# A four-layer gated cross-attention kernel: layer 1's table order turned ahead of the last shared products, and layer 1's last additions moved at the seam to layer 2

## The chip, the cores and the metric

The program runs on one core of a Trainium2 chip. A core has a matrix engine (TensorE, in the profile PE for the products and PEld for the loads of their weights), a vector engine (VectorE, DVE), a scalar engine (ScalarE, ACT), a general engine (GpSimd, POOL) and an engine that only issues transfers here (SyncE, SP). Each takes its instructions in order from its own queue; semaphores order the engines among each other. Transfers (DMA) are started by SP, and the indirect ones, whose addresses come from a table, by POOL. The metric is the device time of one execution in microseconds (us); of three runs the median counts.

## What is computed

Tokens `x` (8 sequences of 256, each token 512 numbers, f32) go through four layers. Each has a cross-attention to `ctx` and a feed-forward part, each behind a layer norm and scaled by the tanh of a gate:

```
x = x + tanh(g_xattn[l]) * xattn_l(layernorm(x), ctx)
x = x + tanh(g_ffn[l])   * ffn_l(layernorm(x))          # l = 0, 1, 2, 3
```

The change lies in layer 1's feed-forward part and at its border with layer 2's attention. These are, cut to what matters:

```
# layer 1, feed-forward: 64 experts, 8 of them for each token, one shared expert for all
def _route(x):                      # scores, the best 4 of 8 groups, the best 8 of their experts
    ...
    return topk_idx, topk_w * 2.5
oh  = one_hot(topk_idx.reshape(-1), 64)
pos = cumsum(oh, 0) - oh            # the place of each choice in its expert's list
buf[e, pos] += x[row]               # tokens gathered by expert
y   = einsum(silu(buf @ w_gate) * (buf @ w_up), w_down)
out = scatter_add(y * weight) + (silu(x @ sh_gate) * (x @ sh_up)) @ sh_down

# layer 2, attention, by sequence of 256 tokens; q = layernorm(x), k = v = ctx
scaled = einsum('bsd,bse->bde', q, k) / sqrt(512)
out    = einsum('bde,bse->bsd', softmax(scaled, axis=1), v)
```

## The kernel before

The 2048 tokens stay on the chip the whole time, as 16 tiles `xt[0..15]` of 128 tokens; four tiles are a block (four blocks, two sequences each). The program is written in the order of the computation, engine by engine; a scheduler lays out each engine's queue from that order, priorities, and explicit edges. `behind(one, other, reason)` is such an edge: `one` is put behind `other`.

*Ahead of the experts (middle, from L646).* For each block of layer 1 the attention runs in two batches (`attend1`, L833); it calls `step(n)` at many places, which moves the routing of earlier token pairs on and issues up to `n` table writes. A "pair" `q` is two tiles; there are eight (0 to 7). `route1(q)` (L969) computes scores, ranks and a payload `pay` (token number and weight) for each of two tiles and eight choices: the payload's weights come from sixteen `hit` products (L1064) on VectorE, and then sixteen `table` writes are pending (L1078). `write(n)` (L945) issues pending writes, each one an indirect DMA on POOL (L950) behind a given matrix product. The table holds, by expert and place, token and weight. The last pair, 7, also computes the order in which the experts come (`ranked`, `ordered`), in which the weights of the experts (`w`, 960 KB for a pair of experts, and `wd`) are then loaded by SP.

The norm of a block (`stats_of` L151, `normed` L169) takes VectorE's statistics, then `rstd` on POOL (L166), then `xn` on VectorE (L174); TensorE turns `xn` over (`tr_f`, L188).

The shared expert (`shared1`, L1087) of a block is 8 products each for gate (`shg`), up (`shu`) and remainder (`shr`), whose products on VectorE give `shT` (L1104; the remainder's two halves L1110), and then 16 products `shd` (L1121) whose results VectorE adds to `x` (`add_scaled`, L221). Blocks 0 to 2 are done here, with pair 7's routing and the pending writes between their steps: three writes at each step (loop at L1162). When all writes are out, POOL waits until they have landed and reads the table in the experts' order (`rows`, L1177); TensorE turns the rows (`who_ps`, L1193, put behind the last shared product), VectorE makes token numbers of them (`who`, L1197, put behind the last shared addition), and POOL gathers the first tokens by them (`xg`, L1213). The expert's first products, `gu`, need the gathered and turned tokens (`tr_xg` on TensorE L188, `eb` on VectorE L102). The experts follow, 112 tiles of gathered tokens, some 500 us. Their results are scattered by token into two buffers.

*Behind the experts.* Block 3's shared expert runs at the end (`end`, L1336). `combine` (L1344) loads the two experts' sums of each tile (`more`, 256 KB, SP) and adds them to `x` on VectorE (L1352): 32 additions. The `more` tiles lie in a ring of eight buffers, so a load waits until an earlier addition has released its buffer. Then layer 2 (`back`, L1552): for sequence `b` the load `kxvs` of 512 KB (L1363), `ctxTc` (1 MB, L91) for a block, the norm of the tokens (`a2`), products `s` of the scores, softmax, products `o`, and additions to `x`. SP issues its loads in order; `behind(... "not before it in the queue")` puts `kxvs` and `ctxTc` behind loads of `more`, and the loads `p` (weights of layer 2's feed-forward part, 512 KB) come after.

Of the kernel before, what the change touches and what calls it, by code (L numbers as in the profile page):

```python
# [11 lines left out]
F32 = mybir.dt.float32  # L12
# [3 lines left out]
ALU = mybir.AluOpType  # L16
# [4 lines left out]
P = 128  # L21
# [5 lines left out]
BLK = 512  # L27
NB = NT // BLK
TB = BLK // P
# [17 lines left out]
def flamingo_kernel(ctx: ExitStack, tc: tile.TileContext, a):  # L47
    nc = tc.nc
# [102 lines left out]
    def stats_of(ts_, name, after=()):  # L151
# [14 lines left out]
        nc.gpsimd.tensor_tensor(out=rstd[:, :n], in0=ve[:, :n], in1=mhalf[:, :n], op=ALU.pow)  # L166
        yield ts_, mv, rstd

    def normed(stats, name, after=()):  # L169
        ts_, mv, rstd = stats  # L170
        out = []
        for i, t in enumerate(ts_):
            xn = xnp.tile([P, C], F32, tag="xn", name=f"xn_{name}_{i}")
            one = nc.vector.tensor_scalar(xn, xt[t], mv[:, i, 0:1], rstd[:, i : i + 1], ALU.subtract, ALU.mult)  # L174
            for other in after:
                behind(one, other, "the scores first")
            out.append(xn)
        return out

    def norm(blk, name):  # L180
# [35 lines left out]
    def mmtile(name):  # L216
        return mm.tile([P, BLK], F32, tag="mm", name=name)

    def add_scaled(i, ps, scale):

        return nc.vector.scalar_tensor_tensor(xt[i], ps, scale, xt[i], ALU.mult, ALU.add)  # L221
# [424 lines left out]
    def middle():  # L646
        with ExitStack() as st:
# [185 lines left out]
            def attend1(blk, one_step):  # L833
# [24 lines left out]
                for bb in range(BLK // S):  # L858
                    nm = f"{blk}_{bb}"
                    kf, V = context1(blk, bb, K, step) if bb else first  # L860
                    if blk == NB - 1 and bb:
                        step = lambda n: one_step(n, True)
                    qf = b8.tile([P, NH // 2, S], F32, tag="b8", name=f"qf_{nm}")
                    for cc in range(2):
# [63 lines left out]
                    for nt in range(2):  # L928
                        aoT = t2.tile([P, KC, P], F32, tag="t2", name=f"aoT_{nm}_{nt}")
                        aoTs.append(aoT)  # L930
                        transpose4(aoT, aos[nt].rearrange("p h d -> p (h d)"), f"ao_{nm}_{nt}")
                        step(1)
                    for nt in range(2):
                        ps = mmtile(f"wo1_{nm}_{nt}")
                        matmul_k(ps, [aoTs[nt][:, k, :] for k in range(KC)], [wo[:, k, :] for k in range(KC)])
                        i = blk * TB + bb * 2 + nt
                        add_scaled(i, ps, tg[:, 1:2])
                        step(2 if nt == 0 else 0)
                    done.append(blk * (BLK // S) + bb)

            tokens, done, counted = {}, [], []
# [27 lines left out]
            def route1(q):  # L969
# [91 lines left out]
                hit = sm.tile([P, E1], F32, tag="hit", name=f"hit{q}", bufs=2)  # L1061
                for i in range(2):
                    for j in range(K1):
                        nc.vector.scalar_tensor_tensor(  # L1064
                            hit, key[:, i, :], key8[:, i, j : j + 1], w[:, i, :], ALU.is_equal, ALU.mult,
                            accum_out=pay[:, i, j, 1:2],
                        )
                    nc.vector.tensor_scalar(
                        pay[:, i, :, 1], pay[:, i, :, 1], den[:, i : i + 1], None, ALU.mult
                    )  # L1070

                    for j in range(K1):
                        pending.append((row_i[:, i, j : j + 1], pay[:, i, j, :]))
                    if q == 2 * NB - 1:
                        write(len(pending))
                    if i == 0 and q == 2 * NB - 1:
                        expert = ranked(run[:, 1, :], sel[:, 1, :])
                    yield  # L1078
                if q == 2 * NB - 1:
                    ordered(expert)  # L1080
                    yield

            I1R = I1 - P
            rows_of = (slice(0, I1R), slice(FD, FD + I1R))
            rest1 = rows_of[1]

            def shared1(blk, shgu):  # L1087


                xnT = [tokens[blk][:, k, :] for k in range(KC)]  # L1090
                hT = [t2.tile([P, BLK], F32, tag="t2", name=f"shT{blk}_{h}") for h in range(2)]
                act = [t2.tile([P, BLK], F32, tag="t2", name=f"sha{blk}_{h}") for h in range(2)]

                def products(name, cols):
                    ps = mmtile(f"{name}{blk}")
                    n = cols.stop - cols.start
                    matmul_k(ps[:n, :], [shgu[:, k, cols] for k in range(KC)], xnT)
                    return ps

                pg = products("shg", slice(0, P))  # L1100
                nc.scalar.activation(act[0], pg, AF.Silu)
                yield
                pu = products("shu", slice(P, 2 * P))
                nc.vector.tensor_tensor(hT[0], pu, act[0], ALU.mult)  # L1104
                yield
                ps = products("shr", slice(2 * P, I1W))
                nc.scalar.activation(act[1][rest1, :], ps[0:I1R, :], AF.Silu)
                for n in range(2):
                    pick = lambda x: x.rearrange("p (t n q) -> p t n q", n=2, q=P)[:, :, n]
                    one = nc.vector.tensor_tensor(  # L1110
                        pick(hT[1][rows_of[n], :]), pick(act[1][rest1, :]), pick(ps[rest1, :]), ALU.mult
                    )
                last_add[:] = [one]
                yield
                for i in range(0, TB, 2):
                    ps = [mmtile(f"shd{blk}_{i + n}") for n in range(2)]
                    last = None
                    for k in range(2):
                        for n in range(2):
                            rows = rows_of[n] if k else slice(0, P)  # L1120
                            one = nc.tensor.matmul(  # L1121
                                ps[n], hT[k][rows, ts(i + n, P)], shd[rows, k, :], start=(k == 0), stop=(k == 1)
                            )
                            if last is not None:
                                behind(one, last, "remainders side by side")
                            last = one
                    latest[:] = [last]
                    for n in range(2):
                        one = add_scaled(blk * TB + i + n, ps[n], tg[:, 5:6])
                        if i + n == 0:  # L1130
                            behind(one, last_add[0], "its place")
                        last_add[:] = [one]
                    yield

            def work():
# [3 lines left out]
                        yield  # L1139
                    yield from route1(q)  # L1140

            last_add = []
            gen = work()

            def step(n, hurry=False):

                for _ in range(2 if hurry else 1):
                    next(gen, None)
                    write(n, latest[0])
# [8 lines left out]
            with tc.high_priority(offset=400):  # L1158
                one = route1(2 * NB - 1)
                for _ in range(3):  # L1160
                    next(one)
            while next(two, 0) is None:  # L1162
                write(3, latest[0])
                with tc.high_priority(offset=400):
                    next(one, 0)
# [26 lines left out]
            for n in range(2):  # L1192
                one = nc.tensor.transpose(who_ps[:, n, :], rows[:, :, n], ident)  # L1193
                if n == 0:
                    behind(one, latest[0], "the table comes late")
            who = l2.tile([P, P], I32, tag="who", name="who")
            one = nc.vector.tensor_copy(who, who_ps[:, 0, :])  # L1197
            behind(one, last_add[0], "the table comes late")
            share = l2.tile([P, P], F32, tag="share", name="share")
            nc.scalar.copy(share, who_ps[:, 1, :])  # L1200

            class Tile:

# [129 lines left out]
            with tc.If(some > PAIRS1):  # L1333
                experts1([(PAIRS1 + E1 + 2 * n, False, (wpool, "w")) for n in range((E1 - PAIRS1) // 2)])

            end = shared1(NB - 1, again)  # L1336
            for _ in range(3):
                next(end)
            first_loads.append(combine(range(2), adds=last_add))
            for _ in end:  # L1340
                pass

# [1 line left out]
    def combine(tiles, after=(), adds=None):  # L1344

        for t in tiles:
            for u in range(2):
                more = t2.tile([P, C], F32, tag="t2", name=f"more{t}_{u}")
                one = nc.sync.dma_start(more, results[u][ts(t, P), :])
                for other in after:  # L1350
                    behind(one, other, "not before it in the queue")
                add = nc.vector.tensor_tensor(xt[t], xt[t], more, ALU.add)  # L1352
                if adds:
                    behind(add, adds[0], "its place")
                    adds[:] = [add]
        return one

    kxvs, kx_load, first_loads = {}, [], []

    def load_kx(b, b8, after=None):  # L1360
        t = b8.tile([P, 4 * C], F32, tag="b8", name=f"kxvs{b}")
# [190 lines left out]
    def back():  # L1552
        with ExitStack() as st:
# [171 lines left out]
            for bb in range(BLK // S):  # L1725
                tiles = (2 * bb, 2 * bb + 1)
                loaded = combine(tiles, kx_load) if bb else first_loads.pop()
                kxvs[bb] = load_kx(bb, bp, loaded)
                xns += norm_of(tiles, f"a2{bb}_")
            context(0, loaded)  # L1730
            first_loads.append(loaded)
            emptied()
# [365 lines left out]
```

## Time and profile before

| | |
|---|---|
| median of three runs | 2705.74 us (2701.91, 2705.74, 2705.78) |
| profiled execution, its own time | 2704.81 us |
| span of the profiled execution | 2703.0 us |
| TensorE clock granted, mean | 0.974 of full speed |
| busy: PE / PEld | 2553.9 us (94%) / 50% |
| busy: DVE | 1288.3 us (48%) |
| busy: POOL | 890.6 us (33%) |
| busy: ACT | 671.9 us |

The table's first rows are times of executions without a profile; the profile shows one execution. In its lines a group of instructions has a line of the program (L1121 is line 1121), an engine, an operation, and `out<-in` by the program's names; the number behind x is how many. "Idle before" is the time in which an engine stood still ahead of an instruction, and behind the arrow is what released it, so `[6.34 <-DMA xg<-xnd,who]` is an engine that waited 6.34 us for that transfer. Stretches show busy time, not work: TensorE works at a granted clock, shown as a share of full speed, and is slower where that is below 1. The stretches that the change touches are 900 to 990 us and 1490 to 1585 us from the start of the span. Some rows of the trace around them:

| row | duration |
|---|---|
| table write on POOL (L950), start to start where nothing holds it | 1.276 to 1.28 us |
| addition of `more` on DVE (L1352), 32 of them | 657 / 684 / 693 ns (least, median, most) |
| four additions 128x512 on POOL (L1426, at 1570.83) | 5.55 us |
| four `xn` on DVE at 1544.59, and at 1570.20 beside those additions | 1.91 us, 3.81 us |
| shared addition on DVE (L221) | 0.75 us |
| `xg` from issue to landing (L1213): least, median, most | 2.8, 4.2, 6.9 us |

### The profile page before, as it was taken

To read this page: it belongs to the slowest core of one execution; us is meant where nothing else is said; L and a number is where in the kernel's file an instruction comes from. 1 tells how busy PE (TensorE), PEld (TensorE's weight loads), DVE (VectorE), ACT (ScalarE), POOL (GpSimd) and SP (SyncE) were. 2 spreads that over 40 slices of the span, in tenths; PEclk is the share of its full clock that TensorE was granted. 3 is DMA by queue.
4 is the path that set the end of the run, shared out by engine and by line. 5 is a ranking of instruction groups with operands and counts; after the bars stand their busy time and mean duration, and the time that the engine had idled before them with its cause. 6 is when DMAs were issued, how large, how long until landed. Compare 5 with 4: busy or idle time off the path is not lost. (4 is left out here: it accounts for less than half of the span.)

```text
span 2703.0 us, 29475 instructions
## 1 busy us (share of the span) xinstructions
PE 2553.9 (94%) x10253; PEld 1355.1 (50%) x10268; DVE 1288.3 (48%) x3535; ACT 671.9 (25%) x1505; POOL 890.6 (33%) x814
## 2 busy tenths in 40 slices
PE   7889898999999899999999899898999999999998
PEld 3445444455665445555555344344454444455554
DVE  7656575536655622222222641767666674121121
ACT  2534344311111113333333211222223231111110
POOL 1111110112444445656565110333333342333332
PEclk9999899999999899999999999999999999999999
DMA  5000000112200259999997721132121211888884
GB/s 214 9 16 24 20 36 4 33 36 63 64 25 25 59 175 237 246 242 246 243 241 169 224 113 64 38 110 61 61 91 67 106 16 47 278 276 270 288 278 113
DMA packets 96187, 333.04 MB, mean 123 GB/s; under 512 B 20608, under 2 KB 23041, under 8 KB 88098
## 3 DMA queue, kind: packets, MB, share of 16 engines
q0 software_dynamic: 45856, 156.51, 23.0%
q1 hardware_dynamic: 47154, 170.34, 18.6%
q10 hardware_dynamic: 3024, 4.25, 0.5%
q8 instruction: 84, 1.38, 0.2%
q14 instruction: 69, 0.57, 0.1%
HBM read 280.46 MB, written 64.91 MB: 128 GB/s over the span
## 5 line engine op out<-in xcount | busy, mean ns | idle before, releaser
L210 PE MATMUL gu<-w,eb 128*128 128x352 f32 x896 | 285.9, 462 | 0.0
L1293 POOL DMA_INDIRECT acc<-eb,who x112 | 177.5, 1585 | 175.5 <-DVE eb L102 148.3
L210 PE MATMUL h2p<-xnT_f,p 128*128 128x512 f32 x512 | 228.0, 601 | 3.0 <-ACT xnT_f L104 3.0
L210 PE MATMUL o2f<-p,h 128*128 128x512 f32 x512 | 224.8, 593 | 0.0
L210 PEld LDWEIGHTS gu<-w,eb 128*128 128x128 f32 x896 | 162.6, 192 | 73.4 <-issue 2.3
L950 POOL DMA_INDIRECT table<-pay,rowi x128 | 126.1, 985 | 120.6 <-issue 26.1
L539 ACT ACTIVATE pr<-pr,n 128x256 f32<-128x256 f32 x256 | 127.9, 501 | 151.7 <-DVE n L534 148.8
L210 PEld LDWEIGHTS h2p<-xnT_f,p 128*128 128x128 f32 x512 | 97.2, 192 | 120.8 <-issue 115.7
L210 PEld LDWEIGHTS o2f<-p,h 128*128 128x128 f32 x512 | 96.2, 190 | 117.4 <-issue 115.2
L1213 POOL DMA_INDIRECT xg<-xnd,who x112 | 117.2, 1046 | 59.6 <-PE ehp L1240 22.8
L221 DVE SCALAR_TENSOR_TENSOR x<-o2f,tg,x 128x512 f32<-128x512 f32 x64 | 47.0, 739 | 140.7 <-PE o2f L210 140.7
L1768 PE MATMUL g_r<-w,xgT 128*128 128x352 f32 x288 | 111.7, 469 | 0.7 <-ACT xgT L104 0.7
L1768 PE MATMUL u_r<-w,xgT 128*128 128x352 f32 x288 | 108.7, 459 | 0.0
L1284 PE MATMUL ed<-w,eb 128*128 128x512 f32 x224 | 105.7, 594 | 0.9 <-DVE eb L1241 0.9
L102 DVE COPY eb<-ed 128x512 f32<-128x512 f32 x56 | 38.7, 692 | 138.6 <-PE ed L1284 138.6
L1775 DVE SCALAR_TENSOR_TENSOR h_r<-a_r,share,u_r 128x352 f32<-128x352 f32 x36 | 20.9, 581 | 175.9 <-PE u_r L1768 167.4
L1791 PE MATMUL d_r<-w,hT_r 128*128 128x512 f32 (+1 forms) x216 | 104.2, 592 | 0.0
L534 DVE CUSTOM_DVE_ANT_0 pr<-s,mask 128x256 f32<-128x256 f32 x256 | 96.9, 417 | 12.2 <-PE s L514 8.8
L1230 DVE SCALAR_TENSOR_TENSOR eb<-eb,share,gu 128x176 f32<-128x176 f32 x112 | 44.0, 393 | 122.0 <-ACT eb L1229 122.0
L591 POOL TENSOR_TENSOR y<-y,gbo 128x512 f32<-128x512 f32 x16 | 20.4, 1272 | 246.8 <-DVE y L590 239.0
L188 PEld LDWEIGHTS tr_xg<-ident,xg 128*128 128x128 f32 x592 | 68.9, 141 | 63.2 <-issue 49.9
L188 PE MATMUL tr_xg<-ident,xg 128*128 128x128 f32 x592 | 92.7, 280 | 6.4 <-DMA xg<-xnd,who 6.3
(534 smaller groups left out, 4730.5 us busy)
## 6 DMA issues: line engine op xcount, KB each, us to landing
w<-in_w SPq DMA_DIRECT2D x64, 960.0 KB, 7.3
p<-in_p SPq DMA_DIRECT2D x64, 512.0 KB, 5.7
xnd<-xn_f SPq DMA_DIRECT2D x32, 256.0 KB, 3.2
acc<-xnd SPq DMA_DIRECT2D x32, 256.0 KB, 4.9
more<-acc SPq DMA_DIRECT2D x32, 256.0 KB, 4.3
wd<-in_wd SPq DMA_DIRECT2D x64, 96.0 KB, 6.9
ctxTa<-in_ctxT SPq DMA_DIRECT2D x4, 1024.0 KB, 6.0
x<-in_x SPq DMA_DIRECT2D x16, 256.0 KB, 5.9
```

The costliest lines, as they stand in the source:

```text
L188: one = nc.tensor.transpose(ps[:, k, :], src[:, ts(k, P)], ident)
L210: one = nc.tensor.matmul(ps, lhsT[k], rhs[k], start=(k == 0), stop=(k == n - 1))
L221: return nc.vector.scalar_tensor_tensor(xt[i], ps, scale, xt[i], ALU.mult, ALU.add)
L534: one = nc.vector.tensor_tensor_reduce(pr[:, nt, :], ps[r][:, nt, :], mask[:, nt, :], -1.0, -LOW, ALU.add, ALU.min, n16[:, nt, h : h + 1],)
L539: nc.scalar.activation(pr[:, nt, :], pr[:, nt, :], AF.Exp, bias=n16[:, nt, h : h + 1], scale=-1.0, accum_out=s16[:, nt, h : h + 1],)
L950: one = nc.gpsimd.indirect_dma_start(out=table[:, :], out_offset=bass.IndirectOffsetOnAxis(ap=rows, axis=0), in_=choice, in_offset=None, b ...
L1213: nc.gpsimd.indirect_dma_start(out=xg, out_offset=None, in_=xnd[:, :], in_offset=bass.IndirectOffsetOnAxis(ap=who[:, c : c + 1], axis=0), ...
L1230: nc.vector.scalar_tensor_tensor(self.h, self.h, share[:, c : c + 1], gu[:, I1 : 2 * I1], ALU.mult, ALU.mult)
L1284: one = nc.tensor.matmul(ps[n], t.hT[rows, k, :], wd, start=(k == 0), stop=(k == 1))
L1293: nc.gpsimd.indirect_dma_start(out=acc[n][:, :], out_offset=bass.IndirectOffsetOnAxis(ap=who[:, t.c : t.c + 1], axis=0), in_=t.x, in_offse ...
L1768: nc.tensor.matmul(ps[:, 0:I3], xTt[:, k, :], wgu[k][:, g, :], start=(k == 0), stop=(k == KC - 1))
L1791: one = nc.tensor.matmul(ps, hT[:cn, n, :], wd[n][:cn], start=(n == 0), stop=(n == 2))
```

## The change

Six edits:

1. In the last block's second batch of layer 1's attention (`quiet`) four places that issued one or two table writes now issue none; the writes stay pending and go out later, with the shared products.
2. The last of the shared expert's remainder products on VectorE (`hidden[0]`) is put ahead of each `hit` sequence's first product where there is one.
3. The loop over the shared steps of blocks 0 to 2 ends one pair of steps earlier (5 × 3 − 2 = 13 steps). The rows are read, turned and made token numbers there, and block 2's products `shd` are put behind the turn of the rows; the rest of the steps follows.
4. `who` is put behind the last remainder product instead of the last shared addition; the edges that kept the shared additions in one place ("its place") are gone.
5. Block 3's four shared additions are not issued in `shared1` but kept (`last_adds`) and put behind the `xn` of the first two tiles of layer 2; its first two accumulators lie in another pool of the accumulator memory (`ac` instead of `mm`).
6. `combine`'s additions for tiles 8 to 15 (16 of 32) go to POOL. The program's queue of SP then has all loads of `more` ahead of `ctxTc` of block 2, `kxvs` of sequence 3, `ctxTc` of block 3, and the seven loads of `p` last; before, two `p` and that `kxvs` stood ahead of those `ctxTc`, and two `p` between loads of `more`.

The number of instructions for the computation is the same.

```diff
     def normed(stats, name, after=()):
...
+        latest_norm[:] = [one]
         return out
...
+                    quiet = blk == NB - 1 and bb
+                    if quiet:
                         step = lambda n: one_step(n, True)
...
                         transpose4(aoT, aos[nt].rearrange("p h d -> p (h d)"), f"ao_{nm}_{nt}")
-                        step(1)
+                        step(0 if quiet else 1)
...
-                        step(2 if nt == 0 else 0)
+                        step(0 if nt or quiet else 2)
...
+                        one = nc.vector.scalar_tensor_tensor(
                             hit, key[:, i, :], key8[:, i, j : j + 1], w[:, i, :], ALU.is_equal, ALU.mult,
                             accum_out=pay[:, i, j, 1:2],
                         )
+                        if hidden and i + j == 0:
+                            behind(one, hidden[0], "the shared expert's first")
...
-            def shared1(blk, shgu):
+            def shared1(blk, shgu, later=None):
...
-                last_add[:] = [one]
+                hidden[:] = [one]
                 yield
                 for i in range(0, TB, 2):
-                    ps = [mmtile(f"shd{blk}_{i + n}") for n in range(2)]
+                    bank, tag = (mm, "mm") if i or later is None else (ac, "ac")
+                    ps = [bank.tile([P, BLK], F32, tag=tag, name=f"shd{blk}_{i + n}") for n in range(2)]
...
+                            if turned:
+                                behind(one, turned.pop(), "the table's order first")
...
-                        one = add_scaled(blk * TB + i + n, ps[n], tg[:, 5:6])
-                        if i + n == 0:
-                            behind(one, last_add[0], "its place")
-                        last_add[:] = [one]
+                        if later is None:
+                            add_scaled(blk * TB + i + n, ps[n], tg[:, 5:6])
+                        else:
+                            later.append((blk * TB + i + n, ps[n], tg[:, 5:6]))
...
-            while next(two, 0) is None:
+            for _ in range(5 * (NB - 1) - 2):
+                next(two)
                 write(3, latest[0])
                 with tc.high_priority(offset=400):
                     next(one, 0)
...
                     behind(one, latest[0], "the table comes late")
+            turned.append(one)
             who = l2.tile([P, P], I32, tag="who", name="who")
             one = nc.vector.tensor_copy(who, who_ps[:, 0, :])
-            behind(one, last_add[0], "the table comes late")
+            behind(one, hidden[0], "the table comes late")
...
+            for _ in two:
+                pass
...
-            end = shared1(NB - 1, again)
+            end = shared1(NB - 1, again, last_adds)
...
-            first_loads.append(combine(range(2), adds=last_add))
+            first_loads.append(combine(range(2), adds=hidden))
...
-                add = nc.vector.tensor_tensor(xt[t], xt[t], more, ALU.add)
+                add = (nc.vector if t < 2 * TB else nc.gpsimd).tensor_tensor(out=xt[t], in0=xt[t], in1=more, op=ALU.add)
...
                 xns += norm_of(tiles, f"a2{bb}_")
+                other = latest_norm[0]
+                for add in last_adds:
+                    behind(add_scaled(*add), other, "layer 2's first tokens first")
+                last_adds.clear()
```

## The prediction

> **What bounds the kernel now.** Four views, in this order. First the stretches of the span with each engine's busy time (columns: stretch, length, then busy time and instruction count of PE, PEld, DVE, ACT, POOL; PE's clock; DMA share; GB/s).
>
> ```profile
> 925.00:945.00 20.00, 16.60 (x34) 5.92 (x33) 14.74 (x82) 0.59 (x1) 9.73 (x11) 0.76 0.01 1
> 965.00:985.00 20.00, 13.66 (x39) 5.85 (x38) 4.55 (x8) 1.00 (x3) 4.80 (x5) 0.87 0.82 265
> 1100.00:1400.00 300.00, 300.00 (x1206) 173.44 (x1205) 82.55 (x200) 95.43 (x230) 177.13 (x135) 1.00 0.96 246
> ```
>
> In layer 1's experts TensorE is busy 300.00 of 300 us at clock 1.00. So whatever brings its first expert product forward ("gu", 985.76) brings the experts forward by as much, and nothing there takes it back. The two seams, 900–990 (shared expert and table order ahead of the experts) and 1490–1585 (into layer 2), are where TensorE idles. Second, what PE waits for in each of them:
>
> ```profile
> PE tr_xg L188 <- DMA xg<-xnd,who: 6.3, 1, 6.3
> PE tr_f L188 <- DVE xn_f L174: 5.3, 1, 5.3
> PE shd L1121 <- DVE shT L1110: 3.4, 1, 3.4
> ...
> PE s L210 <- DVE xn_a__0_12283 L174: 5.2, 1, 5.2
> PE shg L210 <- DVE run L1616: 3.3, 1, 3.3
> PE s L210 <- DMA kxvs<-in_ctx: 2.0, 1, 2.0
> ```
>
> The first seam holds 15.0 us of waits, the second 10.5. Third, the timeline at the first seam (start, duration, instruction, and in brackets its idle time and releaser):
>
> ```profile
> 914.49 0.97 POOL L950 DMA_INDIRECT table<-pay,rowi  x1 [0.30 <-issue]
> 915.48 0.75 POOL L166 TENSOR_TENSOR rstd_f<-ve_f,mhalf 128x2 f32<-128x2 f32 x1
> 916.96 1.94 PE L188 MATMUL tr_f<-ident,xn_f 128*128 128x128 f32 x8 [5.32 <-DVE xn_f L174]
> 957.75 0.97 POOL L950 DMA_INDIRECT table<-pay,rowi  x1 [0.30 <-issue]
> 964.76 1.02 POOL L1177 DMA_INDIRECT rows<-table,row_c  x1 [6.03 <-DMA table<-pay,rowi]
> 977.01 0.51 PE L1193 MATMUL who_ps<-ident,rows 128*128 128x128 f32 x2
> 983.86 1.97 PE L188 MATMUL tr_xg<-ident,xg 128*128 128x128 f32 x8 [6.34 <-DMA xg<-xnd,who]
> ```
>
> POOL writes the table, then rstd; the last write (957.75) is seen landed only at 964.8; who_ps stands behind the 16 shd products (971.17, 5.91 us), though its rows landed at 967.56.
>
> **The change, part by part.** Times are the old trace's clock.
>
> *First seam: writes after rstd.* Eight table writes of pair 6 no longer stand ahead of rstd. ve is done at 911.0 (start 910.83, 0.17), so rstd runs at 911.1 instead of 915.48: −4.4 us for xn and tr_f. TensorE then idles about 1 instead of 5.32. After 5.32 its first eight transposes took 1.94 us; eight take 1.02–1.04 at full clock, and shg's last two 1.92 instead of about 1.0. So shd starts 6.6 earlier, 923.1 instead of 929.70 (4.4 + 0.9 + 0.9 + rest in lgp_f).
>
> *Remainder products ahead of the hits.* DVE did the second shT remainder at 936.74, behind sixteen hits of about 0.34 us; PE waited 3.40 for it and its ten products then took 7.20 instead of ten times 0.43 = 4.3. Both go: 3.4 + 2.9 = 6.3 more, of which I take 5.9, so shd ends at 930.7 instead of 943.2. In the way now: the hits queue behind two products (2 × 0.42) and between them four shared adds (4 × 0.75 = 3.0). Pair 7's payload then is ready at 936.2, as before; POOL wants it only at 939.2 (below), which is the cover. Without it each late microsecond lands on POOL one to one.
>
> *The writes, still 32.* The eight moved ones are not gone: 8 × 1.276 (the pitch in the timeline, 913.22 to 914.49) = 10.2 us now lie in POOL's idle times of 4.67, 2.23 and 3.99 us, all on PE or on the hits. Fifteen of pair 6 go behind the shared products: the first three run 916–920, then 29 remain without a gap: 920.1 + 29 × 1.276 + 0.6 = 957.7, against 958.72. POOL is thus the bound of this stretch and gains only 1 us. But the shared products' weights loads (issued from 956.18 on, 960 KB each, landing 5.3 to 6.8) start with order_ps, 13.5 earlier at 942.6, and are over by 950.5. The last write had 6.03 to wait beside them; in the quiet stretch a write landed in 2.1. So the rows read goes at 959.7 instead of 964.76 and, with its own 2.8, lands at 962.5 instead of 967.56. Bounds: with 6.0 again, 966.4; with 2.1, 962.5. I take the latter, because by then no load of weights moves.
>
> *who_ps ahead of the 16 products.* TensorE has ended shr2 by 957.8 (971.2 less 13.4) and now idles for 4.7 at who_ps; behind it in its queue stand the 16 shd products and, behind those, tr_xg. who_ps runs at 962.5 instead of 977.01, the who cast (0.28) follows at once, since the last four adds no longer stand ahead of it, and xg is issued at 963.6 instead of 978.99. Issue to PE took 4.87, so xg is there at 968.5; the 16 products (5.9, or about 9 if the idle costs what it cost after 3.40, 2.9) end at 969.0 to 972. tr_xg so waits little, and gu, whose first eight took 4.72 instead of 2.53 after the 6.34 idle, saves 2.2 as well. DVE does the four adds (2.8) ahead of the copy of tr_xg, beside PE. gu starts 12 to 16 earlier; floor if the rows are no earlier than before: who_ps at 967.6, 9.4 before its old place, less a colder clock, −7. I take **−14** for this seam.
>
> A page speaks to the idle at who_ps: the Trainium skill, "TensorE: Matmul & The Clock Gate", Part 1: The HAM clock gate, says that TensorE falls to half clock after an idle window of about 3.4 us and needs as long to recover. The rows above agree at 5.32 and 3.40; by it the 16 products cost 3 us more and the seam would be −11 rather than −14, if nothing else covered them.
>
> *Second seam: deferred adds.* DVE's four shared adds (0.75 at 1509.57, 2.06 for three at 1512.63) go behind the first two tokens' xn. xn0 comes at 1513.45 instead of 1516.67 (three adds, 2.06, and about 1.1 of queue), so s starts 3.2 earlier, and its idle of 5.25 shrinks to 2.0. But the second pair's xn now stands behind four adds (3.0) and their statistics: 1524.45 instead of 1523.90, with PE ready at 1521.7. It waits 3.7 there and s's second half starts at 1525.3 instead of 1527.04. What reaches o is **−1.7**.
>
> *Sixteen combine adds to POOL.* On DVE they took 684 ns each. The nearest POOL rows are 1272 ns (y with gbo, 16 of them) and these:
>
> ```profile
> 1543.17 1.38 POOL L166 TENSOR_TENSOR rstd_a<-ve_a,mhalf 128x4 f32<-128x4 f32 x1 [19.31 <-DVE ve_a L164]
> 1551.27 0.39 SPq L1363 DMA_DIRECT2D kxvs<-in_ctx  x1
> 1557.27 3.24 PE L210 MATMUL s<-xn_a,kxvs 128*128 128x512 f32 x7 [1.98 <-DMA kxvs<-in_ctx]
> 1570.20 3.81 DVE L174 TENSOR_SCALAR xn_f<-x,mv_f,rstd_f 128x512 f32<-128x512 f32 x4 [0.46 <-POOL rstd_f L166]
> 1570.83 5.55 POOL L1426 TENSOR_TENSOR x<-x,gb 128x512 f32<-128x512 f32 x4 [0.66 <-DVE xn_f L174]
> ```
>
> The second of them: 1.39 each, while the same four xn on DVE take 3.81 instead of the 1.91 of 1544.59. POOL's order is three adds, then block 1's rstd, then thirteen. That rstd waits for ve, about 1542 and so ends near 1543.3; all later adds wait behind it. SP's order is now all sixteen loads of more, then ctxTc2, kxvs3, ctxTc3, and then p (seven). The loads' ring lets the last go when the eighth POOL add is done: 1543.3 + 5 × 1.3 = 1549.8. kxvs3 is issued near 1550.7, behind 1 MB of ctxTc2 (2.8 us at the 368 GB/s of that stretch), and lands near 1557.5, where before it came at 1557.27. PE, 1.7 earlier there, waits some 3.7 instead of 1.98: the gain is given back. If the clock falls as after 3.40, add 2.9. Bounds: landing as soon after issue as before (6.0) and no contention, 1555.7, −1.6; each of the eight adds slowed by one DVE instruction (0.7), 5.6 late, +5. I take the middle with half of the clock's price: **+1.5**.
>
> The rule that speaks against this part: the Trainium skill, "SBUF — State Buffer", Who interferes with whom, says that GpSimd and VectorE share a port pair as an exclusive lock, and that a VectorE instruction with two SBUF inputs contends with GpSimd's reads. By it both engines' adds go one after the other; the sum would end at the +5 above. The xn row above agrees in kind.
>
> *The rest at nothing:* the two shd accumulators in another PSUM pool, and the dropped ordering edges between shared adds, add no instruction; DVE has 5.26 us of idle at 1507–1517 around them, and would pay 0.75 for each add in the wrong place.
>
> **Sum:** −14 + 1.5 = −12.5. On the profiled execution's 2704.81 (span 2703.0, 1.8 around it) that is 2692.3; that execution lies 0.9 below the median 2705.74, within the 3.9 that the runs spread.
>
> **Rivals.** What a measurement of this kernel can tell from no change is about 0.2%, 5.4 us.
> *Both seams gain.* kxvs3 lands by 1555.7 and the clock holds: −14 − 3.5 = −17.5, 2687.3. For it: DVE is relieved of 16 × 0.684 = 10.9 us. Against: loads run at 338–368 GB/s just then. Chance 0.17.
> *The rows are not earlier.* The last landing stays near 6, or a weights load moves with it: −7 + 1.5, 2699.3. For it: write landings of 5.7 to 6.1 beside loads. Against: those loads end before. Chance 0.19.
> *Seam gains cancelled:* −7 and +5 together, 2702.8, no change. Chance 0.07.
> *POOL's queue turns the sign.* The eight writes cost POOL their full 10.2 because its waits for PE and the hits (some 11) stay: last write ends at 969, rows land at 972.6 to 977. gu comes about T + 9 to T + 12 after rows at T, against T + 18.2 before (985.76 − 967.56); from T = 975 on nothing is left, and at 980 it is 5 late: with +1.5, 2711. For it: POOL already bounds this stretch. Against: pair 6's payload is ready at 905, so nothing of its own holds those writes. Chance 0.07.
> *The forecast*, 2692.3, own range 2688 to 2697: chance 0.50.
>
> **How the numbers follow.** Faster than 2700.3: forecast, both seams, and most of the third case, 0.50 + 0.17 + 0.16 = 0.83. Within: 0.07 and the rest of that case, 0.10. Slower: 0.07. The range 2686 to 2701 leaves out the last two cases and a little below.
>
> **What would show it.** Right: rstd_f directly behind ve_f; tr_f's idle near 1; no wait of shd for shT; the rows read 2 us behind the last write; a new wait of who_ps for rows of 4 to 5; tr_xg's wait under 2; gu near 972; at the second seam two short waits of s in place of one, and a wait for kxvs3 of about 4. Wrong: POOL gaps between its 29 writes, rows later than 967, or kxvs3 beyond 1562.

## The result, and the profile after

| | before | changed |
|---|---|---|
| median | 2704.13 us (7 runs, 2700.86 to 2705.78) | 2695.34 us (7 runs, 2694.03 to 2697.22) |
| ratio of times, 95% interval | | 0.9968 (0.9959 to 0.9977) |
| profiled execution: time, span | 2704.81, 2703.0 us | 2696.55, 2694.8 us |

The changed kernel is 8.8 us faster by the medians; the interval allows 6 to 11. Forecast was 2692.3, 12.5 below the profiled execution; the changed kernel's profiled execution is 8.3 below it. The sign, the seam that pays and the seam that does not were forecast; the first seam gained less than its 14.

First TensorE's waits in the changed kernel (what waits, for what, us in total, times, longest), 880 to 985 us, then 1480 to 1590:

```profile
PE tr_xg L191 <- DMA xg<-xnd,who: 3.0, 1, 3.0
PE who_ps L1204 <- DMA rows<-table,row_c: 2.5, 1, 2.5
PE tr_f L191 <- DVE xn_f L176: 0.9, 1, 0.9
PE shd L1130 <- DVE shT L1118: 0.8, 1, 0.8
...
PE s L213 <- DMA kxvs<-in_ctx: 4.3, 1, 4.3
PE shg L213 <- DVE run L1630: 3.3, 1, 3.3
PE s L213 <- ACT E L1401: 3.1, 1, 3.1
PE s L213 <- DVE xn_a__0_12279 L176: 2.4, 1, 2.4
```

At the first seam tr_f waits 0.9 instead of 5.3 and shd 0.8 instead of 3.4; who_ps is the new wait, 2.5; tr_xg still waits 3.0 for the gathered tokens. At the second, one wait of 5.2 for xn became two of 2.4 and 3.1, and the wait for kxvs rose from 2.0 to 4.3. (The 3.1 is put down to E, yet the second pair's xn, 1514.89 to 1515.44, is what came just before s at 1515.54.) Now the timeline of the first seam in the changed kernel:

```profile
912.41 0.72 POOL L166 TENSOR_TENSOR rstd_f<-ve_f,mhalf 128x2 f32<-128x2 f32 x1 [7.85 <-DVE ve_f L164]
928.05 6.48 PE L1130 MATMUL shd<-shd,shT 48*128 48x512 f32 x10 [0.77 <-DVE shT L1118]
934.46 4.81 PE L213 MATMUL shg<-xnT_f,rwsh 128*128 128x512 f32 x8
959.10 0.97 POOL L954 DMA_INDIRECT table<-pay,rowi  x1 [0.30 <-PE shu L213]
962.12 1.02 POOL L1188 DMA_INDIRECT rows<-table,row_c  x1 [2.05 <-DMA table<-pay,rowi]
964.98 0.33 SPq L113 DMA_DIRECT2D w<-in_w  x1
965.01 0.50 PE L1204 MATMUL who_ps<-ident,rows 128*128 128x128 f32 x2 [2.51 <-DMA rows<-table,row_c]
966.11 1.03 POOL L1227 DMA_INDIRECT xg<-xnd,who  x1 [2.97 <-DVE who L1209]
974.28 2.25 PE L191 MATMUL tr_xg<-ident,xg 128*128 128x128 f32 x8 [3.02 <-DMA xg<-xnd,who]
976.32 3.23 PE L213 MATMUL gu<-w,eb 128*128 128x352 f32 x8
```

rstd now stands alone. The last write starts at 959.10 and is landed 2.05 us after its own 0.97, no longer 6.03. But SP starts loads of expert weights at the very moment at which the rows have landed (964.98), and the gather issued 1.1 us later takes 8.2 to TensorE (966.11 to 974.28) where the old one took 4.9. (The old one was not alone either: 306 GB/s moved between 979.77 and 983.19. But the last load of 960 KB had then been issued 5.1 us ahead of the gather, at 973.89.)

The executions differ ahead of any edit: the last group of qf products starts at 890.04 before and at 891.37 here, between 889.41 and 892.20 in all ten profiles outside one slower session (the middle group of the experiments). So times in the table are counted from that group (start of each row less the start of that qf, worked out from the timelines). change_again, u_turn, u_quiet, u_hidden and w_xg are experiments told below.

| us after the last qf | before | changed | change_again | u_turn | u_quiet | u_hidden | w_xg |
|---|---|---|---|---|---|---|---|
| tr_f | 26.9 | 22.5 | 22.5 | 22.5 | 26.9 | 22.5 | 22.5 |
| shd of block 0 | 39.7 | 32.9 | 32.9 | 32.9 | 39.6 | 32.9 | 32.9 |
| rows read | 74.7 | 70.8 | 70.8 | 70.8 | 75.4 | 71.1 | 70.8 |
| who_ps | 87.0 | 73.6 | 73.6 | 76.8 | 78.2 | 74.4 | 73.6 |
| xg issued | 89.0 | 74.7 | 74.7 | 78.8 | 79.4 | 76.7 | 74.7 |
| tr_xg | 93.8 | 82.9 | 82.1 | 86.7 | 86.9 | 85.1 | 79.8 |
| gu, first | 95.7 | 85.0 | 84.5 | 89.5 | 89.3 | 88.1 | 82.0 |
| shg behind the experts | 604.4 | 592.2 | 591.8 | 598.1 | 597.3 | 597.4 | 588.8 |
| h2p in layer 2 | 690.5 | 681.1 | 680.2 | 687.0 | 685.0 | 685.0 | 677.4 |
| end of the span | 1813.0 | 1803.4 | 1803.1 | 1809.7 | 1806.2 | 1803.5 | 1800.0 |

The first seam brings 10.8 at gu and 12.2 at the end of the experts (gu's first products ran warmer). Between there and h2p 2.8 are lost again (2.4 in change_again). From h2p to the end the kernels take 1118.5 to 1124.5 without being different there: one profile cannot settle 3 us, so stages are read from the traces and totals from the medians.

### The profile page after: what moved, and what is told of

It is laid out like the page before. It is cut to its first block, busy times and chain, and to the rows that moved or that the text cites. A ratio compares the mean times of both kernels' runs of the same rounds, so it can differ in the third digit from the quotient of the medians.

```text
span 2694.8 us, 29464 instructions
## 1 busy us (share of the span) xinstructions
PE 2549.0 (95%) x10253; PEld 1352.6 (50%) x10268; DVE 1286.5 (48%) x3519; ACT 671.6 (25%) x1505; POOL 911.2 (34%) x830
## 3 DMA queue, kind: packets, MB, share of 16 engines
q1 hardware_dynamic: 47154, 170.34, 18.9%
## 5 line engine op out<-in xcount | busy, mean ns | idle before, releaser
L1466 ACT ACTIVATE h<-h2p,b 128x512 f32<-128x512 f32 x64 | 43.2, 687 | 221.4 <-PE h2p L213 221.2
```

## The experiments

Three groups. Beside the first four the kernel before took 2704.67, beside the last four 2703.76. Beside the middle four it took 2732.14 (33 runs): in their profiles the last qf already starts 20 to 31 us later than in the other ten, so that of these only the second seam is read. The middle and the last group ran on a chip of the same number, so that another chip is not shown to be the reason.

**One edit undone at a time, first seam.** u_turn, who_ps behind the last products again (and `who`, in lines left out here, behind the last shared addition):

```diff
-            for _ in range(5 * (NB - 1) - 2):
-                next(two)
+            while next(two, 0) is None:
...
-            turned.append(one)
...
-            for _ in two:
-                pass
```

> The changed kernel with one part undone: who_ps stands behind block 2's 16 shd products again, and the loop runs over all shared steps before the rows are read. Theory (the rows are what the seam waits for; the turn saves only the part of the 16 products that lies behind the rows' landing, 5.9 us less the idle of 2.5 that who_ps then had): first gu 2 to 4 us later than in the changed kernel's profile, wait of who_ps gone, median 2697 to 2700. Rival (the turn is the bulk of the first seam's gain, as the old trace's 977.01 against 967.56 suggests): gu 6 to 9 later, median 2701 to 2705.

Measured: 2699.85 us (11 runs), 0.9984 (0.9975 to 0.9993). who_ps stands 3.2 later, as the theory has it: 5.9 of products less the idle of 2.5. But those products no longer lie over the gather, and the wait comes back bare:

```profile
978.92 1.11 PE L191 MATMUL tr_xg<-ident,xg 128*128 128x128 f32 x4 [9.42 <-DMA xg<-xnd,who]
```

With the clock that TensorE then loses (half speed for 13.65 us around it), gu is 4.5 later and the experts' end 5.9. The turn is worth 4.5 to 5.9: more than the theory, less than the rival.

u_quiet, the eight writes ahead of rstd again:

```diff
-                        step(0 if quiet else 1)
+                        step(1)
...
-                        step(0 if nt or quiet else 2)
+                        step(2 if nt == 0 else 0)
```

> The changed kernel with the eight table writes of pair 6 issued in the attention's last batch again, ahead of rstd. Theory (TensorE loses 4.4 at rstd and some 2 of clock, of which the 2.5 that who_ps waits for the rows absorbs a part): who_ps released by the last shared product rather than by the rows, gu 3 to 5 later, median 2698 to 2700. Rival (POOL alone bounds the seam, so an earlier xn is worth nothing and eight writes off its queue are a gain): gu no later or earlier, median 2693 to 2696.

Measured: 2698.41 us (7 runs), 0.9978 (0.9967 to 0.9989); gu 4.3 later. The size is the theory's, the sign by which it was to be known is not: who_ps is still released by the rows (2.3). The rows themselves are 4.6 later, because the hits of pair 7 now stand behind the shared remainder, that behind xn, and POOL waits for them:

```profile
941.87 0.97 POOL L954 DMA_INDIRECT table<-pay,rowi  x1 [8.67 <-DVE hit L1068]
```

POOL is the bound, but the chain rstd, xn, shT, hits, writes is what paces it. So the rival falls: an earlier xn is worth 4.

u_hidden, without the edge in front of the hits:

```diff
-                        if hidden and i + j == 0:
-                            behind(one, hidden[0], "the shared expert's first")
```

> The changed kernel without the edge that puts pair 7's hits behind the shared expert's remainder products on VectorE. Theory (TensorE's clock falls there with and without the wait, and who_ps waits 2.5 for the rows anyway): shd waits about 3 instead of 0.8 for shT, the wait of who_ps shrinks to about 0, gu 0 to 1.5 later, median 2695 to 2697. Rival (the 5.9 us that the prediction put on this part count in full): gu 5 to 6 later, median 2700 to 2701.

Measured: 2697.3 us (11 runs), 0.9981 (0.9972 to 0.999). shd waits 3.40, who_ps waits no more and is only 0.8 later, so the slack swallowed the wait as expected. gu is nevertheless 3.2 later: `who` stands behind the last remainder product of block 2, which is that much later, so xg goes 2.0 later, and tr_xg waits 4.53. Neither expectation held; the slack covered who_ps but not the edge behind it.

**The loads that meet the gather.** w_xg takes the changed kernel and lets the weights from the third pair on wait for the first gather:

```diff
-            table_read.append(load)
...
-                    nc.gpsimd.indirect_dma_start(
+                    one = nc.gpsimd.indirect_dma_start(
                         out=xg,
...
+                    if not table_read:
+                        table_read.append(one)
```

> The changed kernel with one edit of its own: the loads of the experts' weights from the third pair on wait for the first gather xg instead of for the table's read. Theory (the first gather took 8.2 us from issue to TensorE because six loads of weights start with the rows' landing, 4.9 without them): tr_xg's wait of 3.0 falls under 0.5, TensorE's clock stays at 1.00 there, gu 3 to 4.5 earlier, median 2691 to 2692. Rival (a gather this soon behind the rows takes 8 us by itself): tr_xg waits 3 as before, median 2695. Rival (the later loads starve the third pair): a new wait of gu for w of 3 or more, median 2696 to 2700.

Measured: 2691.78 us (5 runs), 0.9957 (0.9943 to 0.997). The gather in w_xg's timeline:

```profile
965.76 1.03 POOL L1226 DMA_INDIRECT xg<-xnd,who  x1 [2.96 <-DVE who L1208]
969.17 0.33 SPq L113 DMA_DIRECT2D w<-in_w  x1
970.85 1.09 PE L191 MATMUL tr_xg<-ident,xg 128*128 128x128 f32 x8
```

The same issue is now followed by tr_xg after 5.1 us, with no wait and warm. The gather had landed by 969.17, 3.4 after its issue, when SP's load, which waits for it, went out; the rest of the 5.1 is TensorE's 16 products. gu is 3.0 earlier and nothing starves behind it. The collision is shown.

**The second seam**, in the slower session. u_pool puts the adds back (`add = nc.vector.tensor_tensor(...)` for all tiles), u_defer drops `last_adds` from the call of `shared1`; kx_early keeps both and moves loads behind kxvs of sequence 3:

```diff
-            loaded = combine(range(2 * TB, TT))
+            combine(range(2 * TB, 13))
+            loaded = combine(range(13, TT), kx_load)
```

`both` is w_xg and kx_early together.

u_pool, expected:

> The changed kernel with the 16 combine additions of tiles 8 to 15 on VectorE again (684 ns each instead of about 1.3 us on POOL). Theory (POOL's additions behind the second rstd hold the ring of more and so kxvs of sequence 3: 4.3 us of wait and 1.7 of clock at the third group of scores): kxvs comes relatively earlier, its wait is 2 to 3 and the clock holds, from o to h2p some 2 to 3.5 us less, median 2692 to 2693.5. Rival (VectorE's 10.9 us of additions stand in the way again and take back what the deferred shared additions gained): o or s later by as much, median 2695 to 2697.

u_defer, expected:

> The changed kernel with block 3's four shared additions at their old place, in the shared expert's own steps, ahead of layer 2's first xn. Theory (the deferral brings s 2.9 and o 2.4 forward against the old order, and everything up to kxvs of sequence 3 hangs on o): s 3 later, o 2 to 2.5 later, and as much at the end: median 2697 to 2698. Rival (the wait for kxvs of sequence 3 swallows it): o later, o of the second batch not, median 2695 to 2696.

kx_early, expected:

> The changed kernel with one edit of its own: the loads of more for tiles 13 to 15 stand behind kxvs of sequence 3 in SP's queue, so that kxvs waits for two of POOL's additions instead of eight and not behind ctxTc. Theory (that queue place is the whole of the 4.3 us wait and of the 1.7 of clock after it): wait for kxvs under 1, the third group of scores 7.1 us instead of 8.8, h2p 5 to 6 earlier, median 2689.5 to 2690.5. Rival (the transfers themselves bound it: about 0.37 MB per us, with four loads of p now ahead of kxvs): a wait of 2 to 4 stays, median 2693 to 2695.

both, expected:

> The changed kernel with both edits: later weights behind the first gather, and kxvs of sequence 3 ahead of the last loads of more. Theory (the two seams are independent, each shift carried to the end): the sum, 3.6 of the first and 5 to 6 of the second, median 2685.7 to 2687. Rival (one of them is taken back behind the seam, in the clock or in layer 2's loads): 2689 to 2692.

Measured, against 2732.14: u_pool 2727.94, 0.9983 (0.9964 to 1.0002); u_defer 2728.73, 0.9988 (0.9973 to 1.0004); kx_early 2726.12, 0.9977 (0.9963 to 0.9991); both 2722.07, 0.9964 (0.9948 to 0.9981). The changed kernel did not run there, and the totals do not tell these apart. So three more and the changed kernel ran on one chip: first_seam (u_pool and u_defer together), both_again, and best, which adds to `both`, in layer 2's normalisation:

```diff
-            nc.gpsimd.tensor_tensor(out=xt[t], in0=xt[t], in1=gb2, op=ALU.add)
+            one = nc.gpsimd.tensor_tensor(out=xt[t], in0=xt[t], in1=gb2, op=ALU.add)
+            tc.add_manual_dep(one.ins, latest_norm[0].ins.name, ..., reason="the last token first")
```

change_again, expected:

> The changed kernel itself, so that the three others are compared with it on one chip. Every theory: some 9 us below the kernel before, ratio 0.996 to 0.998.

first_seam, expected:

> The changed kernel without its second-seam half: the shared additions of block 3 at their old place and all combine additions on VectorE, the first seam as changed. Theory (the second half costs: from the last shared up product to h2p the changed kernel took 82.3 us, the kernel before 80.9): that stretch takes 80.5 to 81, and the time is 1 to 2 us below the changed kernel's. Rival (the deferral pays in executions in which the clock holds behind kxvs): 1 to 2 us above the changed kernel's.

both_again, expected:

> The changed kernel with the later weights behind the first gather and kxvs of sequence 3 ahead of the last loads of more, beside the changed kernel on one chip. Theory (3.0 to 3.6 at the first seam; at the second 5.4 at the second group of o and 3.2 of it given back at tr_f, so 2.1): 5 to 6 us below the changed kernel's. Rival (the second seam gains nothing on the whole): 3 to 3.6 below.

best, expected:

> As the last, and POOL's additions of gb in layer 2 wait for the last of the block's four normalised tiles, in all four blocks. Theory (the new wait of tr_f, 2.4, comes from xn_f taking 3.8 us beside POOL's additions instead of 1.9 alone): xn_f 1.9 for four, tr_f's wait under 0.5, h2p 2 to 3 earlier, 2 to 3 us below the kernel with two edits. Rival (xn_f is slow for another reason): xn_f still 3.8, no difference. Rival (POOL's additions and the rstd behind them come late and hold the next block's norm): xn_f 1.9, and a new wait of s for xn_a of 1 to 3.

Measured, against 2703.76: change_again 2694.45, 0.9968 (0.9957 to 0.998); first_seam 2694.18, 0.997 (0.9959 to 0.9982); both_again 2689.14, 0.9953 (0.9939 to 0.9966); best 2691.82, 0.9966 (0.9952 to 0.9979). The stretch of the second seam, from the last block's first shu product to h2p, from the starts in each timeline:

| us | before | changed | change_again | first_seam | u_pool | u_defer | kx_early | both_again | best |
|---|---|---|---|---|---|---|---|---|---|
| shu to s | 18.0 | 15.1 | 15.2 | 18.6 | 15.1 | 18.6 | 15.1 | 15.1 | 15.2 |
| s to o | 16.7 | 17.2 | 17.2 | 16.7 | 17.2 | 16.8 | 17.2 | 17.2 | 17.2 |
| o to the second o | 29.8 | 33.7 | 34.7 | 28.9 | 31.9 | 30.0 | 28.3 | 28.3 | 28.3 |
| second o to h2p | 16.3 | 16.3 | 16.3 | 16.3 | 16.6 | 17.5 | 19.6 | 19.9 | 20.1 |
| sum | 80.9 | 82.3 | 83.4 | 80.5 | 80.8 | 82.9 | 80.2 | 80.5 | 80.7 |

The deferral is worth 2.4 at o against the kernel before, and 2.9 between first_seam and u_pool (35.3 and 32.3). From o to h2p the changed kernel then takes 50.0 (change_again 51.0), u_pool 48.4 and first_seam 45.2: more than the gain is lost there, and 1.6 to 2.6 of it go with the move to POOL. In the changed kernel:

```profile
1532.90 17.31 POOL L1366 TENSOR_TENSOR x<-x,more 128x512 f32<-128x512 f32 x13
1540.20 0.42 SPq L91 DMA_DIRECT2D ctxTc<-in_ctxT  x1
1540.71 0.38 SPq L1377 DMA_DIRECT2D kxvs<-in_ctx  x1
1547.51 8.80 PE L213 MATMUL s<-xn_a,kxvs 128*128 128x512 f32 x16 [4.27 <-DMA kxvs<-in_ctx]
```

Thirteen additions of 1.33 us stand behind the rstd; kxvs is issued 7.8 us into them, behind 1 MB of ctxTc, and its products start 6.8 later; these, after the wait, took 8.80 instead of 7.10. In kx_early wait and slow products are both gone: the queue place was the cause.

Which part of that place it was is less clear. In u_defer kxvs is issued as late behind o (18.9 us, 18.2 in the changed kernel) but ahead of ctxTc, and s starts 4.3 after the issue, released by E after an idle of 2.30. In u_pool kxvs is ahead of ctxTc too, but right behind five loads of `more` issued within 3.4 us, and s starts 6.1 after the issue. In both late cases a megabyte or more went out just ahead; no run separates that from the place behind the eighth addition.

The deferral's 3 us are swallowed there, as the rival had it: 82.9 against 82.3 and 83.4 (from shu to the start of the third group of s, ahead of what the clock does, 58.5 against 57.4 and 58.5). u_pool's stretch is 1.6 to 2.6 shorter than the changed kernel's, under or at the low end of the theory's 2 to 3.5, since the wait of 2.5 still cost the clock (8.80, where u_defer's 7.11 came after an idle of 2.30; the last section says what differs).

The moved additions also slow VectorE beside them: the four xn behind that rstd took 1.49 each in the changed kernel, and 0.54 in u_pool and first_seam.

first_seam's stretch is 1.9 to 2.9 shorter (its wait is 1.2, its products 7.11), but its total is no different from the changed kernel's: the medians do not show what the trace does.

kx_early's 5.4 to 6.5 at the second o came as expected, and 3.2 of them (3.6 in both_again) were given back, most of it by a new wait of tr_f for xnT_f, 2.4; in both_again that tr_f also took 1.91 instead of 1.04. The theory for it was that xn_f on VectorE meets POOL's additions. First both_again, then best:

```profile
1555.38 3.82 DVE L176 TENSOR_SCALAR xn_f<-x,mv_f,rstd_f 128x512 f32<-128x512 f32 x4 [0.54 <-POOL rstd_f L166]
1556.01 5.55 POOL L1441 TENSOR_TENSOR x<-x,gb 128x512 f32<-128x512 f32 x4 [0.66 <-DVE xn_f L176]
1562.92 1.91 PE L191 MATMUL tr_f<-ident,xn_f 128*128 128x128 f32 x8 [2.39 <-DVE xnT_f L102]
```

```profile
1555.31 1.92 DVE L176 TENSOR_SCALAR xn_f<-x,mv_f,rstd_f 128x512 f32<-128x512 f32 x4 [0.54 <-POOL rstd_f L166]
1557.31 4.95 POOL L1441 TENSOR_TENSOR x<-x,gb 128x512 f32<-128x512 f32 x4 [2.03 <-DVE xn_f L176]
1563.27 1.00 DVE L176 TENSOR_SCALAR xn_a<-x,mv_a,rstd_a 128x512 f32<-128x512 f32 x2 [2.19 <-POOL rstd_a L166]
1565.63 15.67 PE L213 MATMUL h2p<-xnT_f,p 128*128 128x512 f32 x32 [3.40 <-issue]
```

Kept apart, the four xn_f take 1.92 instead of 3.82, and POOL's four additions 4.95 instead of 5.55: the meeting is shown, and three quarters of its price are VectorE's (1.90 of 2.50). The wait of tr_f falls from 2.39 to 0.68. But rstd_a stands behind those additions; VectorE waits 2.19 for it at xn_a, the last copy of xnT_f behind that (1564.85, 0.68) ends at 1565.53, and h2p starts at 1565.63 after 3.40 (for which the profile names no releaser). That is the second rival of the expectation in kind, with the new wait at h2p instead of s, and best is no better than both_again. both_again is the fastest version found, 5.3 us below the changed kernel by the medians on one chip (2686.31 to 2692.24 against 2690.91 to 2695.98). That is its theory's 5 to 6, though the runs of each spread over 5 us and more.

## Why the prediction was right, and which term was off

The kernel got faster at the seam that was to pay, and lost a little at the other, as forecast. Up to h2p the profile gains 9.4 of the 12.5: 1.8 are missing at the first seam (12.2 for 14) and 1.3 at the second (2.8 lost for 1.5). Of the signs named ahead, the rows read 2 us behind the last write, tr_f's wait, the two short waits of s and kxvs's wait of about 4 came. shd still waited (0.8), who_ps waited 2.5 instead of 4 to 5, tr_xg 3.0 instead of under 2, gu stood at 975 on the old clock instead of 972, and POOL's writes had a gap.

- *rstd behind ve.* Forecast −4.4 for tr_f, wait near 1: −4.4 and 0.9. shd −6.6 forecast, −6.7 measured. u_quiet gives the part its worth: 4.3 at gu.
- *Remainder ahead of the hits.* Mis-sized. The wait went (3.40 to 0.77), but not the price of the clock: ten products took 6.48 instead of 7.20, not 4.3, and shg 4.81 instead of 4.88, not 3.6. I took 5.9 for the wait and the ten products and 0.9 for shg; 3.4 (2.2 and 1.2) did not come. It went out of who_ps's idle, forecast 4.7 and measured 2.5, and cost little: in the slower session, where the ten products took 4.34, the rows were read only 0.3 to 0.4 earlier after qf. Before, the second remainder product stood behind ten hits, not sixteen, with other short instructions between them.
- *The writes.* The last write was forecast to end at 957.7 and ended at 958.7 (960.07 less the 1.3 of the start), because POOL's gaps were 2.1 and not 0.6: at 930.80 a write waited 2.14 for a shd product. Its landing came as in the quiet stretch, 2.05, so the rows read came 1.1 later than forecast.
- *The gather.* The failed term. I took 4.87 from issue to TensorE, as before, and looked for colliding loads only at the last write. The third pair's loads wait for the rows' landing, so whatever brings the rows forward brings them against xg; before, the gather stood 11 us behind that landing (978.99 and 967.56). Measured 8.17. With the 1.2 by which xg was issued late that is 4.5, of which the cover of the 16 products took some; gu came 10.8 instead of 14 earlier. w_xg removes the collision alone and gets 3.0 back. The 3 us that the prediction worked out from the page's idle window for these products did not come: the idle was 2.51, and they took 5.91 as before.
- *Second seam.* s 2.9 earlier (3.2 forecast), o 2.4 (1.7), wait for kxvs 4.27 (3.7), the clock's 1.7 (half of 2.9): sum +1.5 from shu to h2p, forecast +1.5. The other 1.3 of the 2.8 lie ahead of it, in shg (6.5 instead of 5.2 from shg to shu). change_again has 5.1 there, but +2.6 from shu to h2p; so the two profiles agree on 2.4 to 2.8 for the whole, and that the one hits the forecast to the tenth is luck. The rule quoted against moving additions to POOL (the Trainium skill, "SBUF — State Buffer", Who interferes with whom) is borne out only in kind: the sentence quoted is about VectorE instructions with two SBUF inputs, and what slowed beside POOL's additions here is xn, with one tensor as input (3.82 against 1.92, and 1.49 each against 0.54). The +5 did not come: the additions moved to POOL took 1.33 each (17.31 for 13), against 1.27 in the row of before.

Of the rivals, none took the forecast's place: the rows read came 4.0 earlier, kxvs did not come in time, and POOL's gaps, a sign of the last rival, stayed at 2.1.

## What to carry to other kernels

When a wait is shortened, look at what else is released by the same event: here the loads of weights were tied to the rows' landing, harmless until the gather followed the rows at once. Tie bulk transfers to the last small transfer of a chain, not to one in its middle. And an engine with spare time is not free for work that holds a ring of buffers: 16 additions moved off VectorE delayed the loads that the next products waited for; check what each moved instruction releases, not only what it occupies.

## What the runs showed of the hardware

- TensorE's clock changes on a grid of 3.413 us. In all 14 profiles it is 1.0 or 0.5, and each stretch between two changes lasts a whole multiple of that; at half speed 3.41, 6.83, 10.24 or, once, 13.65. A multiple filled with products costs half its length: the 1.7 of the products behind kxvs (8.80 for 7.10) is one, the 3.4 of block 0 (2.2 and 1.2) are two. Three windows of this grid in the changed kernel (stretch, length, busy time and instructions of PE, PEld, DVE, ACT, POOL, then PE's clock, DMA share, GB/s):

```profile
926.49:929.90 3.41, 2.64 (x6) 0.59 (x4) 3.30 (x20) 0.00 (x0) 1.86 (x2) 1.00 0.02 1
929.90:933.31 3.41, 3.41 (x5) 1.00 (x6) 2.90 (x17) 0.00 (x0) 1.94 (x2) 0.50 0.02 3
970.86:974.27 3.41, 0.40 (x2) 0.00 (x0) 1.41 (x2) 0.00 (x0) 0.18 (x1) 1.00 1.04 376
```

  What an idle costs hangs on where it falls. The 2.51 at who_ps lies across two windows, which keep 1.87 and 2.44 us of work, the 3.13 at s across two with 2.24 and 1.45, and the clock stays at 1.00. The 3.02 at tr_xg leaves 0.40 in one window, the 4.27 at kxvs 0.20, and the next window is at half speed. So too the 2.30 of u_defer (1.54 left, products 7.11) and the 2.47 of u_pool (1.03 left, 8.80). In the 14 profiles 173 windows at full clock held under 1.4 us of work, and half speed followed each of them.

  That is not the whole rule: half speed also followed 92 fuller windows. One is the first shown, with an idle of 0.77. In the eight profiles in which that idle began 0.6 to 0.8 us into its window the clock fell; in the four of the slower session it began 2.0 to 3.0 into it, the clock held, and the ten products took 4.34. Why 2.64 us of work were too little there is open. The Trainium skill, "TensorE: Matmul & The Clock Gate", Part 1, names an idle window of about 3.4 us that runs freely; the grid agrees with its length, but a window with 2.64 us of work is not an idle one.
- In the slower session VectorE stood still for 9.5 to 12.2 us ahead of a shared addition, with no instruction of this core named as what released it; in kx_early shg waited 7.2 behind it. What that was is open.
